# A selective scan on one core: tiles of 16 channels by 8 states, with du and delta broadcast out of SBUF

## The chip, the cores and the metric

The kernel runs on one core of one Trainium2 chip. The metric is the device time of one execution in microseconds (us). Three runs of the kernel before gave 11112.75, 11121.65 and 11131.6 us; the median is 11121.65 us.

## The reference, cut to what matters

The input is 8 images of 64 x 64 points and 96 channels. Layer 0 is a normalisation, a projection to 192 channels, a 3 x 3 convolution, and then a selective scan over the 4096 points of an image in four orders (K = 4: row by row, column by column, and both backwards). Layer 1 is an MLP between a spectral upsampling and downsampling. The scan is nearly all of the time, and it is what the change rewrites:

```python
def step(h, inp):
    ul, dl, Bl, Cl = inp
    dA = jnp.exp(dl[..., None] * A)
    h = dA * h + (dl * ul)[..., None] * Bl[:, :, None, :]
    y = jnp.einsum('bkdn,bkn->bkd', h, Cl)
    return (h, y)
```

There are 192 channels (d) with 16 states (n) each, so 3072 independent recurrences per image and order. `delta` (dl) and `du` = dl * ul have one value per channel and point; B and C have one value per state and point; A has one value per channel and state.

## The kernel before, in words

**Tiles.** The scan is cut into chunks of T = 1024 points and, in a chunk, into NT = 24 tiles. A tile has 128 partitions, 8 channels by 16 states, partition 8n + c, and 1024 elements. In all there are 8 images x 4 orders x 4 chunks x 24 = 3072 tiles, in one list; a loop walks it, one tile per step, and emits work for several tiles around it. The tile's number in its chunk, i, gives q = i // 8 (a third of the channels), s = i % 2 and j = (i % 8) // 2.

**What a tile needs.** For tile i these operations are issued:
- `fetch` (L1063, SyncE's queue): `dub` [128, 1024], eight rows of du, each repeated for 16 states. It reads a DRAM tensor `du` in which `prepare` has stored the product. It is issued six tiles ahead; `dub` has four buffers.
- `product_b` (L1069, GpSimd): `bb = dub * br`, three tiles ahead, four buffers. `br` holds B, each state's row repeated for the tile's channels.
- `decay` (L1075, TensorE; L1082, ScalarE): one tile ahead. Two matmuls (four instructions in the profile) with the selection `sel_b` spread eight channels of delta over 128 partitions into `pd` in PSUM; ScalarE then takes the exponential with the scale `neg_a`, in place. `pd` has two buffers.
- `scan` (L1089, VectorE): the recurrence over 1024 points, `pd` and `bb` in, written over `pd`, or, in every third tile (`by_pool`), into `h` in SBUF.
- `product_c` (L1095): `hc = h * cr` with C; on VectorE, and in every third tile on GpSimd, one step later.
- `hold` (L1108): the last column into `carry`, by VectorE, or by ScalarE where the tile is `by_pool`.
- `sums` (L1127, TensorE): every second step, the sum over states for two tiles into `py`, with `sel_r`; after four of them `before`'s rows are added (L1139), `store` copies (L1160) and stores (L1163) the result.

**Preparing a chunk.** `prepare` loads the chunk's 192 rows of u as three thirds (L976), two halves of 512 points on partitions 0 to 63 and 64 to 127; projects them (L987) to `xd`, with B and C among its rows; broadcasts B and C out of `xd` in SBUF into `br` and `cr` (L1004, four transfers of 256 KB); computes delta for each third q (L1012 to L1028) into `dl`; multiplies u by it on GpSimd (L1031) and stores the product to `du` in DRAM (L1034).

**The order.** It is written out by hand: each engine executes its instructions in the order of emission. All DMAs but a few of the start are issued by SyncE (SP), so one that waits there holds back those behind it. In each step the loop emits, in this order, the fetch, GpSimd's products, the next tile's decay, the scan, its product and carry; then `Side.advance` emits pieces of the other stages (the front of the next image, the tail and the MLP of the one before, the preparation of the next chunk) up to a cost per step and engine (`CAPS`); then `turn_over` (L1101) adds one idle matmul where those pieces held less than 1.0 us of TensorE's work.

**Other places the change touches.** In the front, ScalarE copies the convolution's output transposed into `xt` (L589), whole images of 64 or 32 columns, and `lay` (L608, L612) stores them to `u_dram` in pieces of 2 KB or 128 bytes. In the tail, `ye` (L658) loads the row-wise scans' result in pieces of 2 KB into two tiles that hold a whole image, and GpSimd adds it (L684). In the MLP, `t1s`, `t1r`, `xu` and `mq` have five, four, four and three buffers.

Of the kernel before, what the change touches and what calls it, by code (L numbers as in the profile page):

```python
# [8 lines left out]
F32 = mybir.dt.float32  # L9
# [7 lines left out]
DI = 192  # L17
# [119 lines left out]
def kernel(ctx: ExitStack, tc: tile.TileContext, a: dict, out: bass.AP):  # L137
# [32 lines left out]
    for p in range(2):  # L170
# [21 lines left out]
    neg_a = cp.tile([128, K, NT], F32, name="neg_a")  # L192
    queue().dma_start(
        neg_a.rearrange("p k g -> p (k g)"),
        a["a_logs"].rearrange("(c n) k f q j -> n c (k f q j)", n=NS),
    )

    sel_r = cp.tile([128, 4, 32], F32, name="sel_r")
    queue().dma_start(
        sel_r.rearrange("p j m -> p (j m)"), a["sel_r"].rearrange("(c n) j m -> n c (j m)", n=NS)  # L200
    )

    sel_b = cp.tile([128, 8, NS, 8], F32, name="sel_b")
# [67 lines left out]
    def constants_in():  # L271
        nc.gpsimd.memset(xp, 0.0)
        raw["sel"] = tile_([128, 8, 128], "sel_0")
        for hf in range(2):
            nc.sync.dma_start(
                raw["sel"][64 * hf : 64 * hf + 64].rearrange("p j m -> p (j m)"),
                a["sel_b"][0:64, 0:2].rearrange("r q j m -> r (q j m)"),
            )
# [15 lines left out]
    def constants_of_scans():  # L294
        yield {}

        nc.scalar.activation(neg_a, neg_a, AF.Exp)
        nc.vector.tensor_scalar(neg_a, neg_a, -1.0, None, ALU.mult)
        nc.vector.tensor_copy(sel_b, raw["sel"].rearrange("p j (c n) -> p j n c", n=NS))
# [19 lines left out]
    def constants_of_mlp():  # L319
# [95 lines left out]
        cr_ = raw["sel"][:, :3, :]  # L415
# [97 lines left out]
    def front(b):  # L513
# [6 lines left out]
        def begin():  # L520
            yield {}
            pad = v["pad"] = bp.tile([C, W + 2, H + 2], F32, tag="pad", name="pad", bufs=1)
            nc.gpsimd.memset(pad[:, 0, :], 0.0)
            nc.gpsimd.memset(pad[:, W + 1, :], 0.0)
            nc.gpsimd.memset(pad[:, 1 : W + 1, 0:1], 0.0)
            nc.gpsimd.memset(pad[:, 1 : W + 1, H + 1 : H + 2], 0.0)
            v["xt"] = [bp.tile([128, H, w], F32, tag=f"xt{w}", name=f"xt{w}", bufs=1) for w in (W, W // 2)]
            u_dram[b] = [dr.tile([DI, L], F32, tag=f"u{o}", name=f"u{o}") for o in range(2)]
            z_dram[b] = dr.tile([DI, L], F32, tag="z", name="z")
# [40 lines left out]
        def conv(n, g):  # L570
# [5 lines left out]
            for tap in range(9):  # L576
# [11 lines left out]
            xt = v["xt"][n]  # L588
            nc.scalar.copy(  # L589
                xt[:, :, 8 * g : 8 * g + 8].rearrange("p h w -> p w h"), e.rearrange("p (i j) -> p i j", i=8)  # L590
            )
            for rows, cs, blk in parts_of(n, g):
# [3 lines left out]
                )  # L596

        def lay(n):

            yield {}  # L600
            while not all((b, n, blk) in filtered for blk in range(8)):
                yield {}
            for h0 in range(0, H, 8):
                yield dict(dma=262 if n == 0 else 131)
                h1 = h0 + 8
                if n == 0:
                    src = v["xt"][0][:, h0:h1].rearrange("p h w -> p (h w)")
                    nc.sync.dma_start(u_dram[b][0][0:128, W * h0 : W * h1], src)  # L608
                else:
                    u = u_dram[b][0][128:192].rearrange("c (h w) -> c h w", h=H)  # L610
                    for p in range(2):
                        nc.sync.dma_start(u[:, h0:h1, 32 * p : 32 * p + 32], v["xt"][1][64 * p : 64 * p + 64, h0:h1])  # L612
            yield {}
            laid.add((b, n))
# [21 lines left out]
        lays = [(4, 0, lambda n=n: lay(n)) for n in range(2)]  # L636
# [4 lines left out]
        if b == 0:  # L641
            return start + convs[:4], convs[4:] + lays + gates + [bp.close(), bp.close()]
        return start, convs + lays + gates + [bp.close()]

    def tail(b, keep, pairs=True):
# [3 lines left out]
        def begin():  # L649
# [4 lines left out]
            v["ye"] = [bp.tile([C, H, W], F32, tag=f"ye{f}", name=f"ye{f}", bufs=1) for f in range(HF)]  # L654
            for h0 in range(0, H, 8):
                for f in range(HF):
                    yield dict(dma=200)
                    nc.sync.dma_start(  # L658
                        v["ye"][f][:, h0 : h0 + 8].rearrange("p h w -> p (h w)"),
                        y_dram[b][0][f * C : f * C + C, W * h0 : W * h0 + 8 * W],  # L660
                    )
            yield {}
            yield {}

        def block(g):
# [6 lines left out]
            for t, src in zip(yz, (y_dram[b][1], z_dram[b])):  # L672
                for f in range(HF):
# [3 lines left out]
                    )  # L677
            y, z = [yz[0][:, f] for f in range(HF)], yz[1]
            yield {}
            yield {}  # L680
            yield dict(pool=2.6)
            for f in range(HF):
                e = v["ye"][f][:, :, 8 * g : 8 * g + 8].rearrange("p h w -> p w h")
# [102 lines left out]
    def mlp(b, keep):  # L786
# [13 lines left out]
        def up_h(j):  # L800
# [3 lines left out]
            for wh in range(2):  # L804
# [4 lines left out]
                s.append(bp.tile([SIDE, MB], F32, tag="t1s", name="t1s", bufs=5))  # L809
# [9 lines left out]
        def fetch_rows(r0):  # L819
            s = v[r0] = bp.tile([128, 5, C], F32, tag="t1r", name="t1r", bufs=4)  # L820
# [14 lines left out]
        def rows_(r5):  # L835
# [12 lines left out]
            xu = bp.tile([C, px], F32, tag="xu", name="xu", bufs=4)  # L848
            nc.scalar.activation(xu, t[:C, :px], AF.Identity, scale=got["rs"], bias=got["nb"])
            for m in range(3):  # L850
                yield dict(pe=0.95, act=0.7)
                if m == 0:
                    sq = bp.tile([128, 3, px], F32, tag="mq", name="mq", bufs=3)
                t = side.again(n, "ph")
                nc.tensor.matmul(t[:, :px], w1[:, m, :], xu, start=True, stop=True)  # L855
                nc.scalar.activation(sq[:, m, :], t[:, :px], AF.Square, bias=b1[:, m : m + 1])  # L856
            yield dict(pe=0.95)
            t = side.again(n, "p3")
            for j in range(15):
# [3 lines left out]
                    t[:SIDE, C * i : C * i + C], sq[:, m, row], w2q[:, m, :], start=(m == 0), stop=(m == 2)  # L863
# [101 lines left out]
    def prepare(b, k, i0, got):  # L965
# [3 lines left out]
        def begin():  # L969
# [3 lines left out]
            assert k % 2 or all((b, n) in laid for n in range(2))  # L973
            v["u"] = pp.tile([128, Q3, MB], F32, tag="u", name="u", bufs=1)
            for hf, part in enumerate(by_thirds(u_dram[b][k % 2], i0)):
                nc.sync.dma_start(v["u"][64 * hf : 64 * hf + 64], part)  # L976
            got["du"] = dr.tile([DI, T], F32, tag="du", name="du")

        def project():
# [20 lines left out]
            for name, row in (("br", 48), ("cr", 32)):  # L1000
                t = got[name] = pp.tile([128, T], F32, tag=name, name=name)
                for hf in range(2):
                    src = xd[64 * hf + row : 64 * hf + row + NS, None, :]
                    nc.sync.dma_start(t[:, MB * hf : MB * hf + MB], src.to_broadcast([NS, 8, MB]))  # L1004

        def delta(q):
# [13 lines left out]
            if q == 0:  # L1020
                got["dl"] = pp.tile([128, Q3, MB], F32, tag="dl", name="dl")
# [6 lines left out]
            nc.vector.scalar_tensor_tensor(got["dl"][:, q, :], t, 0.0, e, ALU.max, ALU.add)  # L1028
            side.give(n)
            yield dict(pool=1.3)  # L1030
            nc.gpsimd.tensor_tensor(v["u"][:, q, :], got["dl"][:, q, :], v["u"][:, q, :], ALU.mult)  # L1031
            yield {}
            for hf in range(2):
                nc.sync.dma_start(  # L1034
                    got["du"][64 * q : 64 * q + 64, MB * hf : MB * hf + MB], v["u"][64 * hf : 64 * hf + 64, q, :]
                )
            got["ready"] = q == Q3 - 1
# [4 lines left out]
    for b in range(images):  # L1042
        for k in (1, 0, 2, 3):
            order = range(NCH) if k < 2 else range(NCH - 1, -1, -1)
            for n, c in enumerate(order):
                got = {}
                for i in range(NT):
                    q, n8 = divmod(i, 8)
                    s, j = n8 % 2, n8 // 2
                    tiles.append(  # L1050
                        dict(b=b, k=k, i0=c * T, first=n == 0, i=i, q=q, s=s, j=j, g=8 * q + 4 * s + j, got=got)
                    )
# [6 lines left out]
    def fetch(t):  # L1059
        assert t["got"]["ready"]  # L1060
        t["dub"] = sp.tile([128, T], F32, tag="dub", name="dub", bufs=4)
        g = t["g"]
        nc.sync.dma_start(  # L1063
# [289 lines left out]
```

## Time and profile before

| what | value |
|---|---|
| median of three runs | 11121.65 us |
| span of the profiled execution | 11105.8 us; the page gives no other time for it, so what lies around the span is taken as the difference to the median, 15.9 us |
| VectorE (DVE) busy | 10207.5 us, 92% |
| GpSimd (POOL) busy | 10179.6 us, 92% |
| TensorE (PE) busy | 9967.9 us, 90%, of it the decay's products (L1075) 3512.7 us |
| ScalarE (ACT) busy | 5910.6 us, 53%, of it the exponential (L1082) 3340.7 us, 1088 ns each |
| scan (L1089) | 2280 to 2350 ns each |
| product with B on GpSimd (L1069) | 2359 ns each |
| product with C on VectorE and GpSimd (L1095) | 1225 and 2357 ns each |
| DMA queue 1 | 1,042,776 packets, 2391.45 MB, 86.5% of 16 engines' span |
| packets under 512 B | 293,820 |
| HBM read, written | 1929.05 and 328.73 MB |

Engines are named as in the profile. A line such as `DVE pd L1089 <- ACT pd L1082: 113.8, 238, 8.0` says that VectorE's instruction of line 1089 writing `pd` waited for ScalarE's instruction of line 1082: 113.8 us in total, 238 times, 8.0 us at most. In a line on a stretch of time there follow, after the stretch and its length, the busy time and number of instructions of PE, PEld (weight loads), DVE, ACT and POOL, the clock granted to TensorE, the share of the time for which the 16 DMA engines were busy, and their GB/s. A stretch's share counts packets that start in it, so a short one can show over 1.

### The profile page before, as it was taken

How to read it: one execution, taken by the hardware profiler on the slowest of the kernel's cores; microseconds unless marked ns; L12 is line 12 of the kernel's file. 1: busy time of each engine (PE TensorE's matmuls, PEld its weight loads, DVE VectorE, ACT ScalarE, POOL GpSimd, SP SyncE). 2: the span in 40 equal slices, each digit the busy share in tenths (PEclk: the TensorE clock that was granted, in tenths of full speed). 3: DMA queues.
4: the chain of work that ended last, by engine and by line, in shares of the span. 5: the costliest groups of instructions: out<-in, count | busy, mean ns of one | idle time of the engine just before them, and what ended most of it. 6: DMA issues, size and time to landing. Idle time of an engine off the chain costs nothing. (4 is left out here: it accounts for less than half of the span.)

```text
span 11105.8 us, 137238 instructions
## 1 busy us (share of the span) xinstructions
PE 9967.9 (90%) x45020; PEld 3204.6 (29%) x45020; DVE 10207.5 (92%) x7702; ACT 5910.6 (53%) x8218; POOL 10179.6 (92%) x4674
## 2 busy tenths in 40 slices
PE   8898888989889998999889998899988989889988
PEld 2222222322233222332223322233222332223325
DVE  6999999999999999999999999999999999999990
ACT  5455445656455564555545555455554655545543
POOL 5999999999999999999999999999999999999990
PEclk9999999999999999999999999999999999999998
DMA  6888898898988989888988989889898898988981
GB/s 174 215 208 224 209 231 209 217 227 232 233 209 216 225 231 225 212 218 224 240 217 215 224 221 244 209 219 225 217 243 210 217 228 218 247 206 216 227 214 48
DMA packets 1044463, 2401.27 MB, mean 216 GB/s; under 512 B 293820, under 2 KB 314556, under 8 KB 1043752
## 3 DMA queue, kind: packets, MB, share of 16 engines
q1 hardware_dynamic: 1042776, 2391.45, 86.5%
q8 instruction: 361, 5.91, 0.2%
q14 instruction: 350, 2.87, 0.1%
q10 hardware_dynamic: 976, 1.04, 0.0%
HBM read 1929.05 MB, written 328.73 MB: 203 GB/s over the span
## 5 line engine op out<-in xcount | busy, mean ns | idle before, releaser
L1069 POOL TENSOR_TENSOR bb<-dub,br 128x1024 f32<-128x1024 f32 x3072 | 7173.5, 2359 | 208.4 <-DMA dub<-du 149.2
L1082 ACT ACTIVATE pd<-pd,neg_a 128x1024 f32<-128x1024 f32 x3072 | 3340.7, 1088 | 4533.0 <-PE pd L1075 4489.8
L1075 PE MATMUL pd<-dl,sel_b 64*128 64x512 f32 x12288 | 3512.7, 645 | 987.2 <-DVE carry L1108 649.2
L1089 DVE TENSOR_TENSOR_SCAN pd<-pd,carry,bb 128x1024 f32<-128x1024 f32 x1536 | 3610.3, 2350 | 262.2 <-ACT carry L1108 127.9
L1095 POOL TENSOR_TENSOR hc<-h,cr 128x1024 f32<-128x1024 f32 x1024 | 2413.9, 2357 | 352.6 <-DVE h L1089 300.7
L1095 DVE TENSOR_TENSOR hc<-pd,cr 128x1024 f32<-128x1024 f32 x2048 | 2508.4, 1225 | 164.1 <-PE py L1127 20.0
L1075 PEld LDWEIGHTS pd<-dl,sel_b 64*128 64x128 f32 x12288 | 966.7, 186 | 3266.3 <-issue 1511.2
L1089 DVE TENSOR_TENSOR_SCAN h<-pd,carry,bb 128x1024 f32<-128x1024 f32 x768 | 1797.3, 2340 | 5.8 <-ACT pd L1082 5.6
L1127 PE MATMUL py<-hc,sel_r 128*32 128x512 f32 x12288 | 1715.0, 617 | 30.4 <-POOL hc L1095 30.2
L1089 DVE TENSOR_TENSOR_SCAN pd<-pd,bb 128x1024 f32<-128x1024 f32 x512 | 1172.5, 2290 | 98.6 <-ACT carry L1108 75.3
L1101 PE MATMUL idle<-sel_b,ident 128*128 128x512 f32 x1652 | 932.0, 646 | 8.0 <-DVE ty L720 5.9
L562 PE MATMUL pc<-pad,convr 96*128 96x512 f32 (+1 forms) x2304 | 858.3, 616 | 5.7 <-DVE e L585 3.6
L1089 DVE TENSOR_TENSOR_SCAN h<-pd,bb 128x1024 f32<-128x1024 f32 x256 | 583.6, 2280 | 26.0 <-ACT pd L1082 25.2
L1127 PEld LDWEIGHTS py<-hc,sel_r 128*32 128x32 f32 x12288 | 250.3, 109 | 1109.0 <-issue 854.5
L1031 POOL TENSOR_TENSOR u<-dl,u 128x512 f32<-128x512 f32 x384 | 485.0, 1271 | 79.2 <-DVE dl L1028 79.2
L862 PEld LDWEIGHTS p<-w2q,mq 128*100 128x100 f32 x4800 | 452.9, 168 | 274.6 <-issue 214.2
L855 PE MATMUL ph<-xu,w 96*128 96x500 f32 x960 | 504.9, 629 | 11.5 <-ACT mq L856 6.7
L862 PE MATMUL p<-w2q,mq 128*100 128x96 f32 x4800 | 511.5, 258 | 2.3 <-ACT mq L856 2.3
L562 PEld LDWEIGHTS pc<-pad,convr 96*128 96x128 f32 (+1 forms) x2304 | 266.3, 163 | 563.9 <-issue 552.8
L987 PE MATMUL px<-u,xp 64*64 64x512 f32 x1536 | 422.4, 627 | 2.4 <-issue 2.4
L1101 PEld LDWEIGHTS idle<-sel_b,ident 128*128 128x128 f32 x1652 | 249.8, 189 | 596.5 <-issue 522.4
L1012 PE MATMUL pv<-xd,dt_w 64*64 64x512 f32 x1536 | 394.4, 609 | 1.0 <-ACT xd L997 1.0
(153 smaller groups left out, 6707.9 us busy)
## 6 DMA issues: line engine op xcount, KB each, us to landing
dub<-du SPq DMA_DIRECT2D x3072, 512.0 KB
u<-u SPq DMA_DIRECT2D x256, 384.0 KB
du<-u SPq DMA_DIRECT2D x768, 128.0 KB
y<-yq SPq DMA_DIRECT2D x768, 128.0 KB
br<-xd SPq DMA_DIRECT2D x256, 256.0 KB
cr<-xd SPq DMA_DIRECT2D x256, 256.0 KB
yp<-y SPq DMA_DIRECT2D x384, 128.0 KB
yp<-u SPq DMA_DIRECT2D x192, 128.0 KB
```

The source lines that it names most:

```text
L562: nc.tensor.matmul(t[rows].rearrange("p (i j) -> p i j", i=8), weights[:, cs], v["pad"][:, 8 * blk + kw : 8 * blk + kw + 8, kh : kh + H], ...
L855: nc.tensor.matmul(t[:, :px], w1[:, m, :], xu, start=True, stop=True)
L862: nc.tensor.matmul(t[:SIDE, C * i : C * i + C], sq[:, m, row], w2q[:, m, :], start=(m == 0), stop=(m == 2))
L987: nc.tensor.matmul(p[rows], xp[rows, k, q, :], v["u"][rows, q, :], start=(q == 0), stop=(q == 2), skip_group_check=True,)
L1031: nc.gpsimd.tensor_tensor(v["u"][:, q, :], got["dl"][:, q, :], v["u"][:, q, :], ALU.mult)
L1069: nc.gpsimd.tensor_tensor(t["bb"], t["dub"], t["got"]["br"], ALU.mult)
L1075: nc.tensor.matmul(pd[:, MB * hf : MB * hf + MB], sel_b[rows, 4 * t["s"] + t["j"]].rearrange("p n c -> p (n c)"), t["got"]["dl"][rows, t[" ...
L1082: nc.scalar.activation(pd, pd, AF.Exp, scale=neg_a[:, t["k"], t["g"] : t["g"] + 1])
L1089: nc.vector.tensor_tensor_scan(t["h"][:, ::step], pd[:, ::step], t["bb"][:, ::step], 0.0 if t["first"] else held, ALU.mult, ALU.add)
L1095: (nc.gpsimd if t["by_pool"] else nc.vector).tensor_tensor(t["hc"], t["h"], t["got"]["cr"], ALU.mult)
L1101: nc.tensor.matmul(p, ident, sel_b[:, 0:4].rearrange("p j n c -> p (j n c)"), start=True, stop=True)
L1127: nc.tensor.matmul(py[r0 : r0 + 32], sel_r[:, t["j"], :], t["hc"][:, MB * hf : MB * hf + MB], start=(t["j"] == 0), stop=(t["j"] == 3 and t ...
```

## The change

A tile now holds 16 channels by 8 states; `half`, j % 2, says which eight of the 16 states. Tiles m and m + 2 hold the same channels and the two halves.

- `fetch` broadcasts du out of SBUF (`u`, in which the product now stays) to `dub`, each of 16 partitions to eight, in two transfers of 256 KB for two halves of 512 points, once for tiles m and m + 2. The store of du to DRAM is gone.
- A second such fetch, of delta out of `dl`, fills `dlb`. `fetches` says at which step each is issued: dub five steps ahead, dlb three or five. `dub` has four buffers, `dlb` three, each for two tiles.
- `decay` is the exponential alone, reading `dlb` in SBUF and writing `pd` in PSUM. The matmuls and `sel_b` are gone; `rate` finds the column of `neg_a`, which is laid out anew.
- `product_b` writes into `dub` itself for half 1; `bb` has two buffers, for half 0.
- B and C: `prepare` stores `xd`'s 32 rows to DRAM (`bc`); `repeat` loads from there eight states at a time, each row to 16 partitions, 512 KB each: half 0 in `prepare`, half 1 at steps 19 and 22 of a chunk. `br` and `cr` have three buffers each.
- `dl` is one tile per third, five buffers; the last third's delta is held back until step 4 of a chunk.
- `xt` and `ye` are tiles of 16 columns, with pieces of 64 bytes in DRAM, stored and loaded two column blocks at a time; `t1s`, `t1r` and `xu` have one buffer less, `mq` six of a third of the size.

```diff
-    def fetch(t):
-        t["dub"] = sp.tile([128, T], F32, tag="dub", name="dub", bufs=4)
-        nc.sync.dma_start(
-            t["dub"], t["got"]["du"][None, 8 * g : 8 * g + 8, :].to_broadcast([NS, 8, T])
-        )
+    def fetch(m, name, src, bufs):
+        t = tiles[m]
+        t[name] = tiles[m + 2][name] = sp.tile([128, T], F32, tag=name, name=name, bufs=bufs)
+        r0 = 32 * t["s"] + 8 * t["j"]
+        for hf in range(2):
+            rows = src[64 * hf + r0 : 64 * hf + r0 + 16, None, :]
+            nc.sync.dma_start(t[name][:, MB * hf : MB * hf + MB], rows.to_broadcast([16, 8, MB]))
+
+    def fetches(i):
+        m = i + 5
+        if 0 <= m < n and m % 4 < 2:
+            fetch(m, "dub", t["got"]["du"][:, t["q"], :], 4)
+        m = i + 5 - 2 * (i % 2 == 0)
+        if 0 <= m < n and m % 4 == i % 2 ^ 1:
+            fetch(m, "dlb", t["got"]["dl", t["q"]], 3)
...
     def product_b(t):
-        t["bb"] = sp.tile([128, T], F32, tag="bb", name="bb", bufs=4)
-        nc.gpsimd.tensor_tensor(t["bb"], t["dub"], t["got"]["br"], ALU.mult)
+        br = t["got"]["br", t["half"]]
+        t["bb"] = t["dub"] if t["half"] else sp.tile([128, T], F32, tag="bb", name="bb", bufs=2)
+        nc.gpsimd.tensor_tensor(t["bb"], t["dub"], br, ALU.mult)
...
     def decay(t):
-        pd = t["pd"] = psd.tile([128, T], F32, tag="pd", name="pd")
-        for hf in range(2):
-            nc.tensor.matmul(
-                pd[:, MB * hf : MB * hf + MB],
-                sel_b[rows, 4 * t["s"] + t["j"]].rearrange("p n c -> p (n c)"),
-                t["got"]["dl"][rows, t["q"], :],
-            )
-        nc.scalar.activation(pd, pd, AF.Exp, scale=neg_a[:, t["k"], t["g"] : t["g"] + 1])
+        t["pd"] = psd.tile([128, T], F32, tag="pd", name="pd")
+        nc.scalar.activation(t["pd"], t["dlb"], AF.Exp, scale=rate(t))
...
+    def repeat(got, name, half):
+        t = got[name, half] = pp.tile([128, T], F32, tag=name, name=name, bufs=3)
+        r0 = NS * (name == "br") + 8 * half
+        nc.sync.dma_start(t, got["bc"][None, r0 : r0 + 8, :].to_broadcast([NS, 8, T]))
...
-            for name, row in (("br", 48), ("cr", 32)):
-                for hf in range(2):
-                    src = xd[64 * hf + row : 64 * hf + row + NS, None, :]
-                    nc.sync.dma_start(t[:, MB * hf : MB * hf + MB], src.to_broadcast([NS, 8, MB]))
+            bc = got["bc"] = dr.tile([2 * NS, T], F32, tag="bc", name="bc", bufs=3)
+            for hf in range(2):
+                nc.sync.dma_start(bc[:, MB * hf : MB * hf + MB], xd[64 * hf + 32 : 64 * hf + 64, :])
+            for half in range(2 if first else 1):
+                for name in ("br", "cr"):
+                    repeat(got, name, half)
...
-            for hf in range(2):
-                nc.sync.dma_start(
-                    got["du"][64 * q : 64 * q + 64, MB * hf : MB * hf + MB], v["u"][64 * hf : 64 * hf + 64, q, :]
-                )
...
-                    nc.sync.dma_start(u_dram[b][0][0:128, W * h0 : W * h1], src)
+                for rows, cs, blk in parts_of(n, 2 * two):
+                    nc.sync.dma_start(u[cs, h, 8 * blk : 8 * blk + 16], xt[rows, h, :])
...
+                ye = v["ye", g // 2] = bp.tile([C, HF, H, 16], F32, tag="ye", name="ye", bufs=2)
+                        nc.sync.dma_start(
+                            ye[:, f, h0 : h0 + 32, :], src[:, h0 : h0 + 32, 16 * (g // 2) : 16 * (g // 2) + 16]
+                        )
...
-    LEAD, FETCH = 3, 6
+    LEAD, FETCH = 3, 5
```

## The prediction

> **What bounds the kernel now.** I read the page first (sections 1 to 3), then the groups, the waits, busy time by stage, and short stretches of the DMA engines.
>
> ```profile
> span 11105.8 us, 137238 instructions
> PE 9967.9 (90%) x45020; PEld 3204.6 (29%) x45020; DVE 10207.5 (92%) x7702; ACT 5910.6 (53%) x8218; POOL 10179.6 (92%) x4674
> q1 hardware_dynamic: 1042776, 2391.45, 86.5%
> ```
> ```profile
> DVE pd L1089 <- ACT carry L1108: 203.2, 414, 3.6
> DVE pd L1089 <- ACT pd L1082: 113.8, 238, 8.0
> DVE h L1089 <- ACT pd L1082: 30.8, 17, 5.9
> ...
> POOL hc L1095 <- DVE h L1089: 300.7, 335, 6.4
> POOL bb L1069 <- DMA dub<-du: 149.2, 115, 6.0
> POOL bb L1069 <- DVE pd L1089: 46.9, 49, 4.8
> ```
>
> Three resources are nearly full at once: VectorE, GpSimd and the 16 DMA engines. There are 3072 tiles of 3.62 us (11105.8 / 3072). The stretches 0 to 110 and 10830 to 11106 us (386 us) hold no steady scanning; between them VectorE and GpSimd are each about 95% busy. What they lose there is what the waits name: VectorE 347.8 us (203.2 + 113.8 + 30.8) for the exponential, GpSimd the same 347.6 us for VectorE and 149.2 us for the broadcast of du.
>
> The DMA engines decide, so I priced them by stage. Here are stretches in which only br and cr are broadcast, from SBUF, 16 partitions by 2 KB (first five), then stretches of du's present broadcast from DRAM, 4 KB (three), then two with 1024 pieces of 128 bytes. Columns: stretch, engines' busy time, clock, DMA share, GB/s.
>
> ```profile
> 3970.20:3976.70 6.50, 5.41 (x22) 1.49 (x22) 6.11 (x5) 5.70 (x10) 5.81 (x3) 1.00 0.96 190
> 4902.70:4909.00 6.30, 6.30 (x42) 2.99 (x42) 6.03 (x6) 4.14 (x7) 5.39 (x4) 1.00 0.84 190
> 5923.40:5929.80 6.40, 5.19 (x22) 1.38 (x20) 5.93 (x7) 4.50 (x7) 5.54 (x3) 1.00 0.90 205
> 4660.20:4666.50 6.30, 6.18 (x46) 3.34 (x44) 6.20 (x7) 4.24 (x7) 5.77 (x4) 1.00 0.88 185
> 3636.30:3642.70 6.40, 5.01 (x26) 1.67 (x26) 6.30 (x7) 4.34 (x8) 6.40 (x4) 1.00 0.86 203
> ```
> ```profile
> 3976.70:3982.00 5.30, 4.70 (x22) 0.98 (x18) 5.26 (x6) 3.48 (x6) 5.30 (x5) 1.00 0.99 264
> 4909.00:4916.00 7.00, 5.94 (x40) 2.47 (x36) 6.72 (x5) 4.21 (x7) 7.00 (x4) 1.00 1.04 238
> 5930.00:5937.00 7.00, 6.17 (x36) 2.68 (x38) 6.86 (x7) 4.43 (x6) 7.00 (x5) 1.00 0.98 259
> ```
> ```profile
> 9396.00:9398.00 2.00, 2.00 (x8) 0.69 (x6) 1.97 (x2) 1.82 (x2) 1.11 (x2) 1.00 1.19 275
> ```
> ```profile
> 6718.00:6720.00 2.00, 2.00 (x6) 0.68 (x4) 1.90 (x4) 1.64 (x2) 2.00 (x2) 1.00 1.16 246
> ```
>
> The ends, a steady stage, and a stretch in which GpSimd waited for du:
>
> ```profile
> 0.00:110.00 110.00, 83.38 (x272) 36.24 (x274) 29.06 (x88) 41.76 (x75) 12.65 (x26) 0.88 0.39 85
> ...
> 4100.00:5500.00 1400.00, 1266.58 (x5755) 401.89 (x5754) 1324.49 (x994) 767.66 (x1068) 1319.74 (x604) 0.98 0.89 223
> ...
> 10830.00:11106.00 276.00, 236.82 (x1356) 140.81 (x1352) 20.56 (x25) 103.80 (x168) 9.32 (x7) 0.90 0.18 49
> ```
> ```profile
> 4990.00:5040.00 50.00, 42.92 (x214) 16.43 (x214) 49.14 (x39) 24.64 (x39) 44.30 (x22) 1.00 0.99 233
> ```
>
> Price = share x length: the time of all 16 engines together.
> - From DRAM, 4 KB: 19.39 us for 4.88 MB, 3.97 us per MB (whole run: 0.865 x 11105.8 / 2391 = 4.02).
> - From SBUF, 2 KB: 28.34 us for 6.21 MB, of which 5 x 1.049 MB are br and cr; the other 0.97 MB at 3.97 leave 24.5 us: 4.67 us per MB, 18% dearer. The dearest stretch gives 5.25, the cheapest 4.3.
> - 1024 small pieces: 2.38 and 2.32 us less the 0.42 and 0.36 MB beside them: 0.80 us.
>
> **The change part by part.** Times are of all 16 engines; before, they are busy 9607 us.
> 1. du: 3072 fetches of 512 KB from DRAM go (1610.6 MB, -6394). In come 3072 fetches of 256 KB for du and as many for delta, from 16 SBUF partitions each: the same 1610.6 MB at 4.67, +7522. One fetch serves two tiles, but delta is a second tensor, so no byte is saved. The row for br is the same shape, so I take it; bounds 3.97 and 5.25.
> 2. du is no longer stored (768 x 128 KB, -400).
> 3. br and cr now come from DRAM in two halves of states, 512 KB each: -134 MB at 4.67 (-627), +268 MB at 3.97 (+1066), and their own store, 17 MB (+67).
> 4. xt's rows become 64 bytes (393,216 pieces, was 65,536 of 128 bytes and 17 MB of 2 KB), ye's too (393,216, was 25 MB of 2 KB): 720,896 more pieces x 0.80 / 1024 = +563, less 42 MB, -167. Bounds: half and double the price of a piece.
>
> Sum: 9607 - 6394 + 7522 - 400 - 627 + 1066 + 67 + 563 - 167 = 11,237 us, which is 101% of the present span.
>
> 5. TensorE: 6144 decay products (L1075, 3512.7 us) go, busy falls to about 6500 us. The exponential then no longer waits for them; it waits only for delta's broadcast and for its PSUM buffer, which the scan or product two tiles back frees. Those 347.8 us of VectorE's waits are the whole gain; with GpSimd only 5% idle I take half, 174 us, bounds 0 and 348.
> 6. Exponential from SBUF: 1088 ns now from PSUM. ACT is 53% busy; even the SBUF row (L1024, 630 for 512 elements against L1023's 590 from PSUM) adds under 0.1 us a tile. Hidden by the scan (2350).
> 7. Products on GpSimd, scans, products on VectorE, reductions: same count, same shapes, nothing. The odd half's product of du and B is written in place; L1031 is too, at 1271 ns for 512 elements against 2359 for 1024 elsewhere. Twice 1271 is the upper bound: 183 ns x 1536 = 281 us of GpSimd; fixed cost explains it as well, and I take 0.
> 8. New waits. A slot of dub is now freed by the scan of the second tile instead of the product that runs ahead of it, so SP waits for VectorE where it now waits for GpSimd (4445.6 us in all, L1063). Behind it on SP stand dlb, br, cr, yp, the stores and the other stages' loads, so all follow the scan. ACT waits for dlb; carry copies and the other stages' activations stand behind that. VectorE waits, before delta's result is written, for the fetches that read the old one. From slot free to the product that needs it are two tiles, 7.2 us, for 512 KB that cost 2.4 us alone. While the engines have room this hides.
> 9. Constants, smaller buffers of the MLP (t1s, t1r, xu): setup and the last 276 us, nothing; bounds 0 and 30 us.
>
> Path: the DMA engines become the longest. In the two end stretches they work 93 us (0.39 x 110 + 0.18 x 276). For the rest they need 11,144 us. At what share? In steady stages they reach 0.89 to 0.90 now without being the limit; in the stretch 4990 to 5040 us 0.99, with GpSimd at 44.3 of 50. I take 0.98: 11,144 / 0.98 + 386 = 11,757 us of span, and 16 us as the profiled span stands to the median of the runs (11121.65 - 11105.8): 11,770 us. Item 5's gain is covered by the DMA engines and left out.
>
> [...]
>
> **The rivals.**
> - *The DMA engines keep up (faster).* It takes a price of SBUF broadcasts under 4.27 us per MB; there the sum gives today's span. For: the cheapest stretch is 4.3, and other traffic will be mixed in, with 1.3 GB less read from DRAM. Against: the mean of five. Then step 5 pays: 11,106 - 174 + 16 = 10,950, at best 10,770.
> - *Fetches late although the engines have room.* Slots free late, SP in order. The place is GpSimd's product. A late du costs 1.3 us now (149.2 / 115); if every one of 1536 pairs cost that, 1997 us, less the 348 of GpSimd's waits for VectorE: about 12,770. It decides from 0.23 us a pair. Against: two tiles of slack.
> - *TensorE's clock.* After 4 us with TensorE busy 2.09 us (7229 to 7233) the granted clock was 0.50. TensorE would be the limit under 0.585 on average (6500 / 11,106); a slow TensorE is a busier one, so I expect 0.8 to 0.95 and at most 100 us, through late reductions: 11,220.
> - *The change doesn't do what it says:* the changed program has no decay product left, so no.
>
> **How the numbers follow.** Chances: DMA bound 0.60, keeps up 0.27, late fetches 0.09, clock 0.04. DMA bound has its own range: price 4.4 and share 1.0 give 11,100; price 5.25 and share 0.96 give 12,980. My range takes in most of the faster case and stops short of the dearest: 10,870 to 12,800. A measurement can tell 0.2% (22 us) from no change: faster 0.27, same 0.04, slower 0.69.
>
> **What would show it.** Right: DMA share of 0.95 or more in the steady stages, SBUF broadcasts near 4.7 us per MB; GpSimd and ACT waiting on dub and dlb for over 1000 us in all; VectorE and GpSimd at 85 to 88%. Step 5: no ACT wait on a product. Step 4: some 790,000 more pieces under 512 B, 1.0 million in all. Wrong: DMA share under 0.9 with those waits small, or a time under 11,100.

## The result and the profile after

The changed kernel takes 13,988.71 us (median of four runs, 13,970.98 to 14,013.24), against 11,126.62 us for the kernel before in the same comparison: 1.2575 times as long, 95% interval 1.2557 to 1.2593, or 2.86 ms slower. The prediction said slower, by the right engines, and was 2.2 ms too low (11,770); its range ended at 12,800.

From the page of the changed kernel (span, busy time by engine, the DMA queue, the count of packets):

```profile
span 13986.1 us, 114576 instructions
PE 8712.9 (62%) x32816; PEld 2770.2 (20%) x32816; DVE 10199.4 (73%) x7701; ACT 5915.5 (42%) x8219; POOL 10175.3 (73%) x4674
...
DMA packets 2139170, 2449.81 MB, mean 175 GB/s; under 512 B 1057084, under 2 KB 1077692, under 8 KB 2138536
...
q1 hardware_dynamic: 2137560, 2441.47, 86.2%
```

VectorE and GpSimd do the same work as before to within 10 us, in a span 2.88 ms longer: all of the loss is waiting. Queue 1 carries 50 MB more than before and is called no busier (86.2% against 86.5%), but it moves 175 GB/s on average. In engines' time its work rose from 9607 to 12,056 us (0.862 x 13,986.1).

The waits of the changed kernel (engine, line and tile, for whom, us in total, times, longest):

```profile
ACT pd L1090 <- DMA dlb<-dl: 4641.4, 747, 17.2
POOL bb L1082 <- DMA dub<-u: 2818.6, 792, 11.1
...
DVE pd L1097 <- ACT pd L1090: 1141.4, 228, 15.1
...
DVE h L1097 <- ACT pd L1090: 756.4, 179, 11.1
```

Both broadcasts arrive late, and the scan waits behind the exponential. SyncE's own queue does not look like what delays them. The longest entries among its waits, after and before:

```profile
SPq L1067 <- ACT pd L1090: 580.6, 436, 3.0
```
```profile
SPq L1063 <- POOL bb L1069: 4445.6, 2155, 7.0
```

So the requests are out and the transfers are slow, which the first experiment tests. The next lines give the beginning, three steady stretches and the end, and then five stretches in which dub and dlb move alone (by the order of SyncE's requests and the bytes moved since; all pieces of data in them are of 2 KB):

```profile
0.00:110.00 110.00, 78.82 (x246) 34.26 (x248) 25.52 (x83) 34.26 (x63) 7.22 (x22) 0.83 0.41 80
...
4100.00:5500.00 1400.00, 860.70 (x3227) 270.99 (x3228) 1016.12 (x760) 598.03 (x831) 1017.42 (x467) 0.76 0.88 178
6400.00:8100.00 1700.00, 1056.07 (x4036) 336.03 (x4032) 1262.96 (x949) 730.86 (x1017) 1263.17 (x580) 0.76 0.88 179
8500.00:9900.00 1400.00, 860.82 (x3489) 286.33 (x3487) 1064.43 (x792) 607.25 (x852) 1072.43 (x494) 0.77 0.88 182
...
13700.00:13986.00 286.00, 243.40 (x1358) 144.30 (x1356) 14.25 (x21) 104.77 (x171) 7.06 (x7) 0.89 0.22 50
```
```profile
3637.00:3651.00 14.00, 3.87 (x5) 1.22 (x6) 11.14 (x10) 6.66 (x9) 13.67 (x8) 0.50 0.84 153
5347.00:5360.00 13.00, 3.55 (x4) 1.18 (x5) 10.81 (x10) 6.66 (x9) 12.21 (x8) 0.50 0.82 158
7066.00:7080.00 14.00, 3.38 (x4) 1.18 (x5) 10.64 (x10) 6.66 (x9) 13.27 (x9) 0.50 0.84 164
8777.00:8790.00 13.00, 2.05 (x2) 0.50 (x2) 9.01 (x9) 5.90 (x9) 10.93 (x7) 0.50 0.91 178
10490.00:10502.00 12.00, 2.04 (x2) 0.50 (x2) 8.49 (x8) 5.54 (x8) 9.99 (x6) 0.50 0.88 177
```

The steady part runs at a share of 0.88 from end to end, at 178 to 182 GB/s, with everybody waiting for it. Before, a share of 0.89 to 0.90 went with 222 to 225 GB/s and hardly a wait. So the share does not tell full engines from engines with room; here the rate does. The pure stretches show whose rate it is: the five move 153 to 178 GB/s and cost 56.6 us for 10.93 MB, 5.18 us per MB. All such stretches of 5 us and more, 580 with 1.5 us cut from each end, come to 4.6 ms of the trace: 174 GB/s at a share of 0.89, 5.13 us per MB.

### The profile page after: what moved, and what is told of

It is laid out like the page before. It is cut to its first block, busy times and chain, and to the rows that moved or that the text cites. A ratio compares the mean times of both kernels' runs of the same rounds, so it can differ in the third digit from the quotient of the medians.

```text
span 13986.1 us, 114576 instructions
## 1 busy us (share of the span) xinstructions
PE 8712.9 (62%) x32816; PEld 2770.2 (20%) x32816; DVE 10199.4 (73%) x7701; ACT 5915.5 (42%) x8219; POOL 10175.3 (73%) x4674
## 3 DMA queue, kind: packets, MB, share of 16 engines
q1 hardware_dynamic: 2137560, 2441.47, 86.2%
## 5 line engine op out<-in xcount | busy, mean ns | idle before, releaser
L1090 ACT ACTIVATE pd<-dlb,neg_a 128x1024 f32<-128x1024 f32 x3072 | 3411.7, 1114 | 6341.2 <-DMA dlb<-dl 4641.4
L1082 POOL TENSOR_TENSOR bb<-dub,br 128x1024 f32<-128x1024 f32 x1536 | 3612.7, 2352 | 3343.5 <-DMA dub<-u 2818.6
L1135 PE MATMUL py<-hc,sel_r 128*32 128x512 f32 x12288 | 2627.6, 774 | 2608.2 <-POOL hc L1103 2198.6
L1082 POOL TENSOR_TENSOR dub<-dub,br 128x1024 f32<-128x1024 f32 x1536 | 3589.7, 2351 | 0.0
L1097 DVE TENSOR_TENSOR_SCAN pd<-pd,carry,bb 128x1024 f32<-128x1024 f32 x768 | 1803.2, 2348 | 1752.7 <-ACT pd L1090 820.8
L1097 DVE TENSOR_TENSOR_SCAN pd<-pd,carry,dub 128x1024 f32<-128x1024 f32 x768 | 1799.9, 2344 | 32.0 <-POOL dub L1082 16.5
L1109 PE MATMUL idle<-xp,ident 128*128 128x512 f32 x1736 | 1172.6, 781 | 713.1 <-DVE ty L718 293.0
L1097 DVE TENSOR_TENSOR_SCAN h<-pd,carry,bb 128x1024 f32<-128x1024 f32 x384 | 900.1, 2344 | 546.4 <-ACT pd L1090 529.6
L1097 DVE TENSOR_TENSOR_SCAN pd<-pd,bb 128x1024 f32<-128x1024 f32 x256 | 585.7, 2288 | 557.9 <-ACT pd L1090 310.7
L1097 DVE TENSOR_TENSOR_SCAN h<-pd,carry,dub 128x1024 f32<-128x1024 f32 x384 | 898.6, 2340 | 0.3
```

Source lines behind the costliest of these rows:

```text
L1082: nc.gpsimd.tensor_tensor(t["bb"], t["dub"], br, ALU.mult)
L1090: nc.scalar.activation(t["pd"], t["dlb"], AF.Exp, scale=rate(t))
L1097: nc.vector.tensor_tensor_scan(t["h"][:, ::step], pd[:, ::step], t["bb"][:, ::step], 0.0 if t["first"] else held, ALU.mult, ALU.add)
L1109: nc.tensor.matmul(p, ident, xp.rearrange("p k q r -> p (k q r)")[:, :MB], start=True, stop=True)
L1135: nc.tensor.matmul(py[r0 : r0 + 32], sel_r[:, t["j"] // 2, :], t["hc"][:, MB * hf : MB * hf + MB], start=(t["j"] == 0), stop=(t["j"] == 3 ...
```

## The experiments

The runs were made in groups, each beside the kernel before; its medians there were 11,113.86 to 11,126.62 us. Four variants were run once only: the two without delta's broadcast, the one without small pieces and the one with a second idle matmul. The others are medians of four or five runs.

**The source partitions, spread.** A tile's 16 channels are taken 4 partitions apart (4c + g, c = 0 to 15) instead of side by side; the sums over states then write 64 rows of `py` instead of 32, and A's layout follows. Bytes, requests and order stay.

```diff
-        r0 = 32 * t["s"] + 8 * t["j"]
+        g = 2 * t["s"] + t["j"] // 2
...
-            rows = src[64 * hf + r0 : 64 * hf + r0 + 16, None, :]
+            rows = src[64 * hf + g : 64 * hf + 64 : 4, None, :]
...
-                    py[r0 : r0 + 32],
-                    sel_r[:, t["j"] // 2, :],
+                    py[r0 : r0 + 64],
+                    sel_r[:, 2 * t["s"] + t["j"] // 2, :],
```

> One change to the changed kernel: a broadcast's 16 source partitions lie 4 apart (channels 4c + g) instead of side by side; same bytes, same number of transfers, same slots. Theory A (the SBUF broadcasts are dear because 16 neighbouring partitions share few read paths): a 2 KB piece falls from 163 ns towards 84 to 110, the 16 engines' work from 12.1 ms to about 9 ms, GpSimd's and ScalarE's waits for dub and dlb nearly vanish, and the time falls to 10.9 to 11.3 ms. Theory B (fetches are requested too late, slots come free too late): nothing changes, 13.8 to 14.1 ms. Theory C (TensorE's clock): TensorE's sums get longer, 14 ms or more.

11,355.84 us, 1.0211 times before (1.0194 to 1.0228): 2.63 of the 2.86 ms are gone. That is theory A's way, 56 us over its range; the two waits fall, but do not nearly vanish. Its queue, two of its waits, a steady stretch and two stretches of pure broadcasts:

```profile
q1 hardware_dynamic: 2137528, 2441.53, 85.4%
```
```profile
ACT pd L1084 <- DMA dlb<-dl: 928.3, 240, 11.1
...
POOL bb L1076 <- DMA dub<-u: 481.2, 224, 8.1
```
```profile
4100.00:5500.00 1400.00, 1095.74 (x4095) 373.02 (x4094) 1285.70 (x967) 751.39 (x1044) 1293.23 (x594) 0.88 0.89 223
```
```profile
4515.00:4530.00 15.00, 7.74 (x22) 2.49 (x22) 14.68 (x13) 3.54 (x4) 15.00 (x8) 0.77 0.52 142
...
7268.00:7282.00 14.00, 7.09 (x22) 2.30 (x22) 13.72 (x12) 3.35 (x3) 14.00 (x7) 0.76 0.58 161
```

The same 2441 MB now cost 9703 us of the engines (0.854 x 11,361.7) instead of 12,056, and a share of 0.89 carries 223 GB/s where 0.88 carried 178. In the two pure stretches 142 GB/s need a share of 0.52 and 161 need 0.58, 3.7 and 3.6 us per MB (all 411 of this trace: 3.77, at 193 GB/s and 0.73). The engines have room there and GpSimd is busy throughout, where before the spread such stretches took 0.89 for 174 GB/s. A piece of 2 KB then takes one engine some 120 ns, not the 84 to 110 that were expected. The place of the source rows in SBUF was the cause: a second way of spreading them, which leaves the reductions as they were, brings nearly as much (11,446.69 us, below). Theory A's reason for it, few read paths, was the author's conjecture: the runs show that the place of the rows changes the cost (12,056 against 9703 us), and not why. No distance but four was tried.

**Delta's broadcast left out, and then du's requests made earlier.** The first run drops dlb's fetch; the exponential reads B's rows with a constant scale instead, so delta is missing from the recurrence and the output is not the reference's. The second also gives dub five slots and asks seven steps ahead.

```diff
-            fetch(m, "dlb", t["got"]["dl", t["q"]], 3)
+            pass
...
-        nc.scalar.activation(t["pd"], t["dlb"], AF.Exp, scale=rate(t))
+        nc.scalar.activation(t["pd"], t["got"]["br", t["half"]], AF.Exp, scale=eps)
```

> Delta's broadcast is left out: the exponential reads B's rows with a constant scale instead, so the recurrence is not the reference's; all other work is there. Theory A: the engines' work falls by a third to about 8 ms, du's fetches land in time, 10.8 to 11.2 ms; it is also the most that dropping the decay products alone can bring. Theory B: a dub slot still comes free only after a scan, GpSimd still waits some 2.8 ms, 13 ms or more. Theory C: clock unchanged near 0.77, time near 14 ms.

11,229.49 us, a little over the expected range. Delta's half of the broadcasts returns 2.76 ms, but that is not the whole way: the DMA share is 0.76 or 0.77, and still GpSimd waits for dub.

```profile
POOL bb L1082 <- DMA dub<-u: 476.0, 229, 6.7
```
```profile
4100.00:5500.00 1400.00, 1031.97 (x4147) 331.47 (x4148) 1317.18 (x988) 767.59 (x1060) 1317.83 (x604) 0.83 0.76 153
```

The queue's work is 8230 us (its share of 0.733 x 11,227.7), 3826 less for 805 MB: 4.75 us per MB.

```diff
-        m = i + 5
+        m = i + 7
...
-            fetch(m, "dub", t["got"]["du"][:, t["q"], :], 4)
+            fetch(m, "dub", t["got"]["du"][:, t["q"], :], 5)
```

> What is left out: delta's broadcast and delta itself in the exponent, as in the run without delta's broadcast (11,229 us); the output is not the reference's. Against that run one thing differs: dub has five slots instead of four and is requested seven steps ahead instead of five. Theory L (the loss that is left once the engines have room is late requests for du: a slot comes free too late): GpSimd's wait for dub falls from 476 us to under 150 us and the time by 100 to 300 us, to 10,930 to 11,130. [...]

11,040.29 us, 189 less, and the wait is

```profile
POOL bb L1082 <- DMA dub<-u: 98.0, 60, 4.1
```

So there is a second, smaller loss at a share of 0.76: du comes too late for the step at which it is asked for. Asking earlier is one cure. Faster transfers are another: with spread rows and unchanged requests, in a kernel without delta's broadcast (11,164.02 us, below), GpSimd's wait for dub is 67.8 us.

**Decay products back on TensorE, no broadcast of delta.** This undoes the half of the change that put delta on the DMA engines (the matmuls with `sel_b` stand in `decay` again); du is still broadcast out of SBUF.

```diff
-        nc.scalar.activation(t["pd"], t["dlb"], AF.Exp, scale=rate(t))
+        pd, g = t["pd"], 2 * t["s"] + t["j"] // 2
+        for hf in range(2):
+            rows = slice(64 * hf, 64 * hf + 64)
+            nc.tensor.matmul(
+                pd[:, MB * hf : MB * hf + MB],
+                sel_b[rows, g].rearrange("p c n -> p (c n)"),
+                t["got"]["dl", t["q"]][rows],
...
+            )
+        nc.scalar.activation(pd, pd, AF.Exp, scale=rate(t))
```

> The decay products on TensorE are put back (with 16 channels by 8 states) and delta's broadcast is dropped; du stays broadcast from SBUF, once for two tiles. Theory A: DMA work about 8 ms, not the limit; the exponential waits for the product again, so 11.0 to 11.3 ms, at or just under the kernel before. Theory B: over 13 ms. Theory C: the clock returns to 0.95 or more and so does the time of before, about 11.1 ms.

11,388.23 us, 1.0244 times before (1.0229 to 1.0259), over the expected range, and here too GpSimd waits for du, 532.5 us, with the engines 0.76 busy in the stretch 4100 to 5500:

```profile
POOL bb L1093 <- DMA dub<-u: 532.5, 296, 6.8
```

**The same with spread partitions, in two ways.** First with 64 rows to the reduction, as above:

> Against the run with the decay products and no broadcast of delta (11,388 us) one thing differs: the source partitions of a broadcast are 4 apart. Theory L (late requests, an empty engine notwithstanding): faster transfers shorten the lateness but do not end it: GpSimd waits for dub 150 to 400 us (532 before), time 11,200 to 11,350. [...] Rival T (what holds the time here is TensorE, 89% busy, with the products back): no change, 11,350 to 11,420.

11,750.12 us, 1.057 times before (1.0553 to 1.0588): neither theory L nor rival T had it. GpSimd's wait for dub falls from 532.5 to 32.0 us, and the kernel is 362 us slower.

```profile
POOL bb L1087 <- DMA dub<-u: 32.0, 33, 4.4
```

Rival T had named the right engine, but expected no change. The groups of TensorE's reduction tell it, without the spread and with it (the line of busy times is the second kernel's):

```profile
L1156 PE MATMUL py<-hc,sel_r 128*32 128x512 f32 x12288 | 1738.4, 618 | 73.6 <-POOL hc L1124 71.4 <-ACT yq L1189 1.6
```
```profile
PE 11206.4 (95%) x45104; PEld 3694.6 (31%) x45104; DVE 10264.2 (87%) x7705; ACT 5895.9 (50%) x8219; POOL 10206.4 (87%) x4674
...
L1150 PE MATMUL py<-hc,sel_r 128*64 128x512 f32 x12288 | 2994.8, 608 | 11.8 <-POOL hc L1118 11.8
```

One matmul takes as long (618 and 608 ns), the group takes 1.26 ms more: the 32-row matmuls overlap 4.4 deep (12,288 x 618 ns / 1738.4 us), the 64-row ones 2.5 deep (12,288 x 608 ns / 2994.8 us). TensorE, 95% busy, looked like the limit. Two further runs settle it. One gives this kernel dub in five slots, seven steps ahead, as in the diff above:

> The kernel with spread partitions and decay products, with dub in five slots and requested seven steps ahead. Theory L: GpSimd's wait for dub falls under 100 us and the time to 10,900 to 11,100, at or under the kernel before (11,123). [...]

11,786.36 us: no gain from earlier requests. The other spreads the channels when u is loaded, so that `py` keeps its rows and the sums write 32 of them; the weights of `dt_w`, `xp` and the bias are reordered in the host's layout.

```diff
-                nc.sync.dma_start(v["u"][64 * hf : 64 * hf + 64], part)
+                for g in range(4):
+                    nc.sync.dma_start(v["u"][64 * hf + g : 64 * hf + 64 : 4], part[16 * g : 16 * g + 16])
```

> Spread partitions, reductions onto 32 rows, decay products on TensorE, no broadcast of delta. Theory R (the 11,750 us of the same kernel with reductions onto 64 rows came from TensorE alone, 95% busy there): TensorE's busy time falls to 9,950 to 10,200, GpSimd's wait for dub stays under 100 us, and the time is that of the kernel before or below: 10,950 to 11,130. Rival T (TensorE bounds it with either reduction): 11,300 to 11,750.

11,164.02 us, 1.0038 times before (1.0025 to 1.0051); the reduction takes 1698.3 us again, TensorE is busy for 10,029.7, and GpSimd's longest wait is the one for VectorE, as in the kernel before (326.3 and 300.7 us). So TensorE had been the limit with 64 rows. It is 34 us above the expected range. Against the same kernel with neighbouring partitions the spread is worth 224 us; the DMA share in the steady stretches is 0.60 instead of 0.76. It is also far under the 0.89 of the kernel before, and no time is gained on it, which speaks against the engines' having limited that kernel at 0.89. Five slots change nothing here either (11,166.4 us):

> The same with dub in five slots, requested seven steps ahead. With GpSimd's wait for dub already under 100 us, theory L and theory R expect within 40 us of the same kernel with four slots, and the wait under 50 us.

**Pieces of 64 bytes taken out** of the changed kernel, with whole runs of 1 and 2 KB in their place, in the store of `xt` (shown) and the load of `ye`. The transposition of rows and columns is left out with them:

```diff
-                    nc.sync.dma_start(u[cs, h, 8 * blk : 8 * blk + 16], xt[rows, h, :])
+                    nc.sync.dma_start(
+                        u_dram[b][0][cs, MB * blk + 16 * h0 : MB * blk + 16 * h0 + 256],
+                        xt[rows, h, :].rearrange("p h w -> p (h w)"),
+                    )
```

> What is left out: the transposition of rows and columns in the store of xt and the load of ye; the same bytes go to and from whole runs of 1 and 2 KB instead of 64-byte pieces, so the output is not the reference's. All else is the changed kernel (13,989 us). Theory A (the DMA engines set the time, so work taken off them comes back): item 4 prices the pieces at 563 us of the 16 engines; at the share of 0.88 some 0.5 to 0.65 ms less, 13,340 to 13,500. [...]

13,622.64 us, 366 less, where theory A expected 0.5 to 0.65 ms. The queue's line is

```profile
q1 hardware_dynamic: 1387992, 2441.47, 85.2%
```

so its work fell by 451 us (12,056 less 0.852 x 13,620.8 = 11,605) for 749,568 packets fewer, 0.60 ns of all 16 engines each. Most of what is taken off the engines comes back as time. At an unchanged share of 0.88 it would be 512 us; the steady share is 0.87 now, at 183 GB/s.

**TensorE's clock.** A second idle matmul per step, in `turn_over`, to lift the clock:

```diff
-            nc.tensor.matmul(p, ident, xp.rearrange("p k q r -> p (k q r)")[:, :MB], start=True, stop=True)
+            for _ in range(2):
+                nc.tensor.matmul(p, ident, xp.rearrange("p k q r -> p (k q r)")[:, :MB], start=True, stop=True)
```

> Two idle matmuls instead of one in each step that has room, nothing else. The granted clock should rise from 0.77 to 0.9 or more. Theory A and B: time within 1.5% of the changed kernel's 13989 us. Theory C: 11.2 to 12 ms.

14,001.66 us, no change. The clock rose only from 0.769 to 0.793, short of what I expected, so the run does not test a full clock. But TensorE's own waits in the changed kernel speak too:

```profile
PEld py L1135 <- POOL hc L1103: 2731.3, 599, 18.4
PE py L1135 <- POOL hc L1103: 2198.6, 514, 17.5
```

Its reduction stood waiting for GpSimd's product. It was early, not late. And the runs on the full change that got most of the time back, at 11,231 to 11,447 us, did so at clocks of 0.81 to 0.88, not at the 0.98 of the kernel before.

**What is left once the rows are spread.** Five runs on the full change. The spread with 32-row reductions (the fetch's lines of the first diff and the loads of u of the last):

> The changed kernel with a tile's 16 channels 4 partitions apart, as in the run with spread source partitions (11,356 us), but with the channels of u and delta reordered when u is loaded, so that the reductions still write 32 rows each as in the changed kernel, and not 64. Theory R (reductions onto 64 rows cost TensorE about 1.2 ms more, shown by the spread kernel with decay products: 2,995 us in that group against 1,738): TensorE's busy time falls by several hundred us, to 8,000 to 8,500, but TensorE was not the bound there, so the time gains 0 to 150 us: 11,200 to 11,360. [...]

11,446.69 us, 1.0295 times before (1.0278 to 1.0312). TensorE's busy time fell as expected (8894.0 to 8300.1 us), but the time rose by 91 us. TensorE was not the limit here, so nothing was to be had. Where the 91 us come from stays open. ACT waits 1005.6 us for dlb instead of 928.3, but with that wait gone in both kernels (the two runs at the end of this section) 77 of the 91 us remain, and GpSimd waits 67 us longer for du. With dub in five slots and asked for seven steps ahead, as in the diff above, and three buffers of other stages one smaller to make room:

> The kernel before this one with dub in five slots, requested seven steps ahead (three buffers of other stages are one smaller to make room: t2, mq, xt). Theory L (late requests for du): GpSimd's wait for dub falls from about 480 us to under 200 us and the time by 80 to 250 us, to 10,950 to 11,250. Rival (the DMA engines, at a share of 0.89, set the time): no change, within 40 us.

12,261.78 us, 0.8 ms slower, which neither expectation had. Its waits, of ScalarE first and then of SyncE's queue (the fetches stand at L1068):

```profile
ACT pd L1091 <- DMA dlb<-dl: 3145.8, 716, 14.2
```
```profile
SPq L1068 <- DVE pd L1098: 1823.2, 423, 11.7
SPq L1068 <- DVE h L1098: 1111.1, 251, 9.3
```

Dub is now in time (GpSimd waits 25.7 us for it), and delta is late. Five slots do not last for seven steps: every second request must wait for a scan of its own step, SyncE stands there for 2.9 ms, and delta's request stands behind it. One step less, and nothing else changed:

```diff
-        m = i + 7
+        m = i + 6
```

> The kernel with five slots for dub, spread partitions and reductions onto 32 rows (12,262 us), with one thing changed: the request is made six steps ahead and not seven, so that the scan which frees the slot stands a step before the request instead of in the same step. Theory Q (the request for du waits on SP for that scan, and delta's request stands behind it on the same queue: ACT waited 3,146 us for dlb there, 1,006 with four slots): SP's waits for scans fall by over 1,000 us, ACT's wait for dlb to 600 to 1,200 us, and the time to 11,200 to 11,450. Rival (five slots put more transfers in flight, which slow delta's, or the smaller buffers of the other stages cost the time): still 11,900 to 12,300.

11,435.15 us, as theory Q expected. SyncE's waits for scans are 332.0 and 513.5 us, and

```profile
ACT pd L1091 <- DMA dlb<-dl: 1174.0, 283, 11.2
...
POOL bb L1083 <- DMA dub<-u: 169.3, 73, 6.1
```

That the wait on SyncE cost the 0.8 ms is shown; the smaller buffers and the fifth slot are in both kernels. But it also shows that du's lateness alone was not what held this kernel: with 364 us less of it than with four slots (533.6 to 169.3) the time is the same, and ScalarE waits longer for delta. So delta's turn, with four slots and six steps, on the kernel with 64-row reductions (11,355.84 us):

```diff
-        m = i + 5 - 2 * (i % 2 == 0)
-        if 0 <= m < n and m % 4 == i % 2 ^ 1:
+        m = i + 6
+        if 0 <= m < n and m % 4 < 2:
             t = tiles[m]
-            fetch(m, "dlb", t["got"]["dl", t["q"]], 3)
+            fetch(m, "dlb", t["got"]["dl", t["q"]], 4)
```

> The kernel with spread source partitions (11,356 us) with delta's broadcast in four slots and requested six steps ahead of its tile (three slots and three or five steps there; the same three buffers of other stages one smaller). Theory Q (what is left there is late requests for delta, and ACT's 928 us of waiting for it): that wait falls under 400 us and the time to 11,100 to 11,280. Rival (the DMA engines, 0.89 busy in the steady stretches, set the time): 11,330 to 11,400, with the wait moved, not removed.

11,231.2 us, 1.0104 times before (1.0088 to 1.0119), 125 less, inside theory Q's range, with ScalarE's wait for dlb down from 928.3 to 48.8 us.

```profile
POOL bb L1076 <- DMA dub<-u: 427.3, 204, 8.5
...
ACT pd L1084 <- DMA dlb<-dl: 48.8, 23, 3.8
```
```profile
4100.00:5500.00 1400.00, 1100.35 (x4140) 376.10 (x4139) 1311.63 (x984) 765.24 (x1056) 1313.63 (x602) 0.88 0.90 227
```

The engines move 227 GB/s at 0.90 where they moved 223 at 0.89 without this edit: they had not been full. The same change on the kernel with 32-row reductions agrees:

> The same change on the kernel with reductions onto 32 rows (11,447 us, DMA share 0.86). Theory Q: ACT's wait for dlb falls from 1,006 us to under 400 us and the time to 11,150 to 11,350. Rival: within 40 us of 11,447.

11,307.88 us, 139 less, the wait 35.9 us. What is left in the better of the two, 117 us against the kernel before, stands beside GpSimd's 427.3 us of waiting for du (149.2 before); that the one causes the other is not shown. Both broadcasts earlier at once were not tried, so whether the full change can reach the time before stays open. The only run that was faster than the kernel before, 11,040 us, leaves delta out.

## Why the prediction was wrong in size

- **What bounds it, and the direction: right, for a cause that the sum did not hold.** The DMA transfers became the longest; ScalarE and GpSimd wait on dlb and dub as announced (over 1000 us; 7460 us), VectorE and GpSimd fell, to 73% where 85 to 88% was forecast, and no ScalarE wait on a decay product is left. The sign of a DMA share of 0.95 or more did not appear. And what made the broadcasts long was the place of their source rows.
- **The path's share of 0.98: wrong, and the largest error.** It was read from 50 us in which du came from DRAM, and carried over to traffic from 16 SBUF rows. With everybody waiting it was 0.88: (12,056 - 108) / (13,986 - 396), with 108 us of work in the ends (0.41 x 110 + 0.22 x 286). With the measured work, a share of 0.98 gives 12,588 us of span and 0.88 gives 13,973: 1.39 ms of the 2.23 ms. The range took 0.96 as its lowest share, and so could not reach the result.
- **The sum of 11,237 us: 819 too low, worth 0.83 ms.** Item 1's price of 4.67 was 5.13 where the broadcasts moved alone, which makes 0.46 x 1610.6 = 741 us; taking delta's half out gave back 4.75, which makes 129. Part of it was a reading: the five stretches for br and cr hold 2153 pieces of 2 KB, at most 4.41 MB of them, and not the 5.24 MB that were counted; with 4.41 they give 4.81. By item 4's prices the pieces and bytes of the run without small pieces come to 415 us (786,432 pieces at 614, less 50 MB at 200), and it gave back 451, 36 more. That leaves some 40 us (650 by the price of 4.75) that no run assigns; items 2 and 3 were not tried alone.
- **The common root of both.** The five stretches for the price held part of the answer in another column. They moved 185 to 205 GB/s at shares of 0.84 to 0.96. I multiplied share by length, as if the missing 4 to 16% were room that other work could use. In the changed kernel the broadcasts alone run at 174 GB/s and 0.89, with the waits to prove that more was wanted, and the mixture ran little faster, 178 to 182 GB/s: other traffic hardly slipped past. It was not the whole answer: all bytes at the 195 GB/s of those five stretches would have made some 12.8 ms with the ends, an estimate.
- **The place of the source rows: it decided, and no item asks for it.** Item 1's price was read from 16 neighbouring rows, br's and cr's, and the change reads 16 neighbouring rows too. The broadcasts reach 174 GB/s in the pure stretches, which makes 9.3 ms for their 1610.6 MB. With rows four apart they reach 193 GB/s at a share of 0.73 instead of 0.89, and 2.63 ms came back. Why neighbouring rows cost more is not shown.
- **Item 5: covered, as said.** Where delta costs the DMA engines nothing and du comes in time, the time is 11,040 us, 80 under the 11,120 of its comparison, inside the 0 to 348 given. The single run lacks delta, so this is a hint only. TensorE's busy time did not fall to 6500 us but to 8712.9, at a granted clock of 0.769.
- **Item 6 and item 7: right.** The exponential takes 1114 ns from SBUF, hidden; GpSimd's product takes 2351 ns in place and 2352 ns not.
- **Item 8: wrong in part.** "While the engines have room this hides" does not hold: at a share of 0.76 GpSimd waits 476 us for du, and asking earlier gains 189 us. With faster transfers, from spread rows, it does hide (67.8 us). What it says of SyncE's order is right, and was shown at its worst by the run with five slots and seven steps on the full change: 0.8 ms.
- **The rivals.** *The engines keep up* needed a price under 4.27; with the rows spread, the pure stretches give 3.77. *Late fetches although the engines have room* exists beneath the main loss, but at 0.1 to 0.2 ms and not 1.65: GpSimd waited 229 times for dub, not for every one of 1536 pairs. *TensorE's clock* fell lower than I thought, to 0.769, and cost nothing that a run shows.
- **Small terms.** The 16 us put around the span are 1.9 in the runs, each of which lists both (13,988.04 and 13,986.1); 14 us change nothing here. The packets under 512 B rose by 763,264, between item 4's 720,896 and the 790,000 among the signs.

## What to carry to other kernels

Read the rate beside the share: here the broadcasts alone moved 174 GB/s at a share of 0.89, where the kernel before moved 223 at the same share, and the whole traffic of the changed kernel ran little faster than its broadcasts. And a stretch that is to price one kind of transfer must hold that kind alone: count its pieces. For a broadcast out of SBUF, try source rows from partitions that lie apart; here four apart instead of neighbouring was worth 2.6 ms of 14. And before a request is moved earlier on a queue that keeps its order, count the steps its slots last: one step too far cost 0.8 ms, paid by the request behind it.

## What was not expected of the hardware

- A broadcast's cost depended on where its source rows lay: the same bytes in the same pieces cost 12,056 and 9703 us of the engines.
- The share at which the engines were full was not one number: 0.88 at 178 GB/s with 7.5 ms of waits on the two broadcasts, 0.89 at 223 GB/s in the kernel before with 0.15 ms of waits on du.
- Reductions onto 64 rows instead of 32 cost TensorE 1.26 ms more at nearly the same duration of one matmul (608 and 618 ns), by overlapping 2.5 deep instead of 4.4.
- Whole runs in place of 64-byte pieces, 749,568 packets fewer for the same bytes, took 451 us off the 16 engines, 9.6 ns of one engine each.
- A second idle matmul per step lifted the granted clock by 0.024 only.
